# Masked sums inside the experts' work, one select for two heads, and the end stage's buffers in two pools

## The chip, the core and the metric

The kernel runs on one core of a Trainium2 chip. The metric is the device time of one execution in microseconds (us). Five engines follow their own instruction streams: TensorE (PE, with its weight loads shown as PEld), VectorE (DVE), ScalarE (ACT), GpSimd (POOL) and SyncE (SP, which here only issues DMAs). Times inside one execution are counted from the start of the profiled span.

## The reference

One transformer block in float32 on 2048 tokens of width 512. Attention and the feed-forward part both read the normalised input, and both are added to the input.

```python
xn = layernorm(x)
# attention: 16 heads, each with two score maps of width 16
q, k = rotary(xn @ Wq), rotary(xn @ Wk)
attn1 = softmax(causal(q1 @ k1.T * scale)) @ v        # v is 32 wide
attn2 = softmax(causal(q2 @ k2.T * scale)) @ v
f = rfft(attn1, axis=time) - lambda_full * rfft(attn2, axis=time)
attn = irfft(f * exp(-0.5 * (linspace(0, 1, n_freq) / 0.15) ** 2), axis=time)
attn = attn * rsqrt(mean(attn * attn, over each head) + 1e-5) * rms_weight * (1 - LAMBDA_INIT)
# feed forward: 8 experts 352 wide, the best 2 for each token, and a shared one 704 wide
y = sum over the token's 2 experts of weight * (silu(xn @ w1) * (xn @ w3)) @ w2
shared = (silu(xn @ sw1) * (xn @ sw3)) @ sw2
return x + attn @ Wout + y + shared
```

## The kernel before

**Stages.** A first stage normalises the input, routes the tokens to the experts and makes queries, keys and values. The middle stage runs from about 100 to 1240 us: attention on all heads, and between its steps the feed-forward part, so that PE always has one of the two to do. The end stage finishes the filter along time, normalises, multiplies by `Wout` and adds everything up. Middle and end are hand-ordered: PE, DVE, ACT and POOL execute in the order in which the code emits their instructions. Only SP's DMAs are placed by a scheduler.

**Attention.** The heads go in 8 groups `g` of two, and each group in 4 chunks of 512 queries, from the last (`qc` = 3) to the first. A chunk is a list of units. In a unit PE makes a 128 x 2 x 512 tile of scores (`ps_s`, line 822), ACT takes its exponential into a `pt` tile (line 835), PE multiplies `pt` with the values into `ps_o` (line 862), and DVE adds `pt` up into `sum0` or `sum1` for the denominator (lines 876 and 879). Five units of each chunk lie on the diagonal and are masked: POOL zeroes one triangle of 128 columns of `pt` for each part of a unit (the select, line 840). Two of these units cover one key block each for the two heads, two pack two parts, and the last one holds the same key block for both heads, at columns 0 and 256. A group has 29 + 21 + 13 + 5 = 68 units.

**Closing a chunk.** When all units are multiplied, PE sums `sum0` and `sum1` over partitions (line 888), transposes the result, and DVE takes the reciprocal `rcp` (line 903) and scales (`o_n`, line 908). POOL then adds the two maps into `vd` (`put`, line 917). The transposed denominators share PSUM banks with other work of PE, among it the experts' `xy`, so PE can wait for `rcp`.

**Fold steps.** Once a group's four chunks are done, its part of the transform along time is done on POOL by `folded` (lines 928 to 970), a generator with 8 steps of 2, 2, 4, 5, 5, 6, 5 and 3 instructions between its yields. The main loop runs 0, 1 or 2 such steps at the end of an iteration.

**The main loop** takes four units at a time. It emits two units' scores, products with values, the sums of a closing chunk, two more units' scores, more products, the put and the reciprocals of chunks that end; then it alternates `work()`, a step of the generator of the feed-forward part, with `added(...)`, the sums on DVE; last come the fold steps. In each step of `work()` there are DVE instructions of the experts too, and POOL issues the gather `xrow` of the tokens of a coming tile (line 623).

**The end stage** opens the pools `tail1` (the matrices of the filter, `wo_sb`) and `tail` (all else). It begins with the last part of the shared expert: `wh` (PE), `ws` (ACT line 256, DVE lines 257 and 263). Then come products with 23 matrices (`ps_r`, `ps_z`, lines 1141), `first` on ACT (line 1184), the sums `vd` on DVE (lines 1186 and 1187, which combine `ps_r` and `first`), and so on. Meanwhile the residual tiles `res` are prepared for 16 tiles of tokens: SP loads the input (line 1120), POOL issues a DMA that accumulates the shared expert's result `ysh` on it (line 1123) and two indirect DMAs that accumulate the routed experts' rows from `ys` (line 1125). Twelve `res` buffers exist; the last four tiles are prepared as buffers come free (`still`).

**The closing loop** runs over n = 0 to 7, with two tiles of tokens in each round. `prepared(n+2)` makes `y` on DVE (line 1163) and its square `sq` on ACT (line 1219); `means` reduces `sq` to `ms` on DVE (line 1223) and asks ACT for the root; `scales` makes `rms` and then `a` (line 1234) on DVE; `across` transposes `a` on PE (`ps_tr`, line 1262) and copies it to `aT` on ACT (line 1264); `projected` multiplies with `wo_sb` (`po`, line 1270); `finished` adds `po` to `res` on DVE (line 1275) and stores it. At n = 1 the shared expert's last tile is copied out of PSUM (`y_sb`).

A pool's tile at an address waits for all users of older tiles at this address, and the first tile of a pool opened in place of older ones waits for the users of all of the region that the pool covers.

Of the kernel before, what the change touches and what calls it, by code (L numbers as in the profile page):

```python
# [8 lines left out]
F32 = mybir.dt.float32  # L9
# [4 lines left out]
ALU = mybir.AluOpType  # L14
AX = mybir.AxisListType
PSUM = bass.MemoryType.PSUM
# [3 lines left out]
P = 128  # L20
T = 2048
E = 512
# [45 lines left out]
def block_kernel(  # L68
# [527 lines left out]
    def middle(general):  # L596


        with ExitStack() as pools:
# [157 lines left out]
            def greatest(g, qc):  # L757
# [28 lines left out]
                nc.vector.tensor_copy(shift, ps.rearrange("p t q -> p (t q)"))  # L786
                return shift

            class Chunk:


# [19 lines left out]
                def scores(self, unit):  # L811

                    g, qc = self.g, self.qc
                    if general and not self.probs:
                        self.shift = greatest(g, qc)
                    ps = sps.tile([P, 2, QC], F32, tag="sc", name="ps_s")
                    for h, kb, off, col, w in unit:
                        for s in range(2):
                            r = slice(64 * s, 64 * s + 64)
                            k = keys[2 * g + h, kb // TQ][r, kb % TQ * P : (kb % TQ + 1) * P]  # L820
                            to = ps[:, s, col : col + w]
                            nc.tensor.matmul(  # L822
                                to, k, queries[2 * g + h, qc][r, off : off + w], start=True, stop=not general
                            )
                            if general:
                                r = 64 * h + 32 * s
                                nc.tensor.matmul(
                                    to, ones[r : r + 1, :], self.shift[r : r + 1, off : off + w],
                                    start=False, stop=kb < qc * TQ,
                                )  # L830
                                if kb >= qc * TQ:
                                    nc.tensor.matmul(to[:, :P], identb, mask, start=False, stop=True)
                    pt = pp.tile([P, 2, QC], F32, tag="pt", name="pt")
                    used = slice(min(c for *_, c, _ in unit), max(c + w for *_, c, w in unit))
                    nc.scalar.activation(pt[:, :, used], ps[:, :, used], AF.Exp, scale=SCALE)  # L835
                    for _, kb, _, col, _ in unit:
                        if kb >= qc * TQ and not general:

                            part = pt[:, :, col : col + P]
                            nc.gpsimd.affine_select(  # L840
                                out=part, in_=part, pattern=[[0, 2], [1, P]], compare_op=ALU.is_ge, fill=0.0,
                                base=0, channel_multiplier=-1,
                            )
                    ready = []
                    for h, kb, off, col, w in unit:
                        self.probs[h, kb] = pt[:, :, col : col + w], off
                        if (1 - h, kb) in self.probs:
                            ready.append((self, kb))
                    return ready
# [163 lines left out]
            def work():  # L1013
                nonlocal worked
                worked += next(ex, work_all)

            def masked(entry):
                _, c, unit = entry
                return any(kb >= c.qc * TQ for _, kb, *_ in unit)

            def added(entries):

                for n, c, unit in entries:
# [5 lines left out]
            for i in range(0, len(stream), 4):  # L1029
                units = stream[i : i + 4]  # L1030
                found = burst(units[:2])
                n, ended = values()
                for c in closing:
                    c.sums()
                    summed += 1
                if n < 2 and not closing:

                    work()
                found += burst(units[2:])
                while todo:  # L1040
                    ended += values()[1]
                todo += found
                for c in closed:
                    c.put(nc.gpsimd)
                    if c.qc == 0:
                        ready.append(c.g)
                closed, closing = closing, ended
                for c in closed:
                    c.finish()
                held, before = [], held  # L1050
                added(before)
                added(u for u in units[:2] if not masked(u))
                later = [u for u in units[2:] if not masked(u)]
                while True:
                    work()
                    added(later[:1])
                    later = later[1:]
                    if worked / (work_all - left) >= (i + 4) / len(stream):
                        break
                added(later)  # L1060
                added(u for u in units if masked(u))
                if any(map(masked, units)) or not shared:
                    steps = 0
                else:
                    steps = 1 if any(map(masked, stream[i + 4 : i + 8])) else 2
                for _ in range(steps):
                    if folding is None and ready:
                        folding = folded(ready.pop(0), nc.gpsimd)
                    if folding is not None and next(folding, 0) == 0:
                        folding = None  # L1070
# [20 lines left out]
    def ending():  # L1091

        with tc.tile_pool(name="tail1", bufs=1) as t1, tc.tile_pool(name="tail", bufs=2) as tp, tc.tile_pool(
            name="tail_ps", bufs=4, space=PSUM
        ) as fps, tc.tile_pool(name="conv_ps", bufs=2, space=PSUM) as zps, tc.manual_schedule(
            engines={mybir.EngineType.PE, mybir.EngineType.DVE, mybir.EngineType.Activation, mybir.EngineType.Pool}
        ):
            conv = t1.tile([P, CONVS * P], F32, name="conv")  # L1100
            nc.scalar.dma_start(conv[:, : 11 * P], conv_t[:, : 11 * P])
            nc.scalar.dma_start(conv[:, 11 * P :], conv_t[:, 11 * P :])
            _, _, _, _, (_, _, stored), _ = expert(tp, fps)
            hidden, gated, times, _, result = shared_expert(tp, fps, 2)
            fetch_down(wex[NX + 1 : NX + 2], 1, nc.scalar)
            wo_sb = t1.tile([P, NE, E], F32, name="wo_sb")
            nc.scalar.dma_start(wo_sb, wout.rearrange("(c p) e -> p c e", p=P))
# [8 lines left out]

            def fetched(k, step):
                if step == 0:
                    res = tp.tile([P, E], F32, tag="res", name="res", bufs=12)
                    nc.sync.dma_start(res, query[0, order[k] * P : (order[k] + 1) * P, :])  # L1120
                    came.append(res)
                elif step == 1:
                    nc.gpsimd.dma_start(came[k], ysh[order[k]], accum_op=ALU.add)
                else:
                    nc.gpsimd.indirect_dma_start(  # L1125
                        out=came[k], out_offset=None, in_=ys,
                        in_offset=bass.IndirectOffsetOnAxis(ap=slot[:, step - 2, order[k] : order[k] + 1], axis=0),
                        compute_op=ALU.add,
                    )
# [20 lines left out]
                return z  # L1150

            def copied(z):
                diff = tp.tile([P, 2, E], F32, tag="diff", name="diff")
                nc.scalar.copy(diff, z)
                return diff

# [23 lines left out]
            zr = pair("ps_r")  # L1180
            product(zr[:, 0, :], [(0, vd[:, 0, :])])
            product(zr[:, 1, :], [(1, vd[:, 1, :])])
            first = tp.tile([P, E], F32, tag="first", name="first", bufs=1)
            nc.scalar.copy(first, zr[:, 1, :])
            z4 = at(0, fold, 2)
            nc.vector.tensor_add(low[:, 0], zr[:, 0, :], first)
# [86 lines left out]
            def finished(k, po):  # L1273
                res = came[k]
                nc.vector.tensor_add(res, res, po)
                nc.sync.dma_start(out_t[:, order[k], :], res)
# [35 lines left out]
            for n in range(NT // 2):  # L1312
                after = across(2 * n + 1)
                ahead, po = po, projected(aT)
                if n + 1 < NT // 2:
                    pairs[n + 1].scales()
                if n == 1:
                    stored(y, ysh[NT - 1], 0.5)
                if n + 1 < NT // 2:
                    aT = across(2 * n + 2)  # L1320
                if n + 2 < NT // 2:
                    pairs.append(prepared(n + 2))
                if ahead is not None:
                    finished(2 * n - 1, ahead)
                    still(2 * n - 1)
                if n + 2 < NT // 2:
                    pairs[n + 2].means()
                if n + 1 < NT // 2:
                    now, po = po, projected(after)
                    finished(2 * n, now)  # L1330
                    still(2 * n)
# [138 lines left out]
```

## Time and profile before

| | us |
|---|---|
| median of 3 runs | 1359.56 |
| the three runs | 1359.56, 1356.74, 1360.22 |
| the profiled execution | 1360.14 |
| its span, first to last instruction | 1358.3 |
| PE busy | 1312.6 |
| DVE busy | 1005.4 |
| ACT busy | 688.4 |
| POOL busy | 626.3 |
| mean granted clock of PE | 0.994 of full speed |

The profile page and the answers of the trace use lines of this form: start, duration, engine, line, operation, output<-input with sizes, a count, and in brackets the idle time just before with what ended it (the releaser, seen from semaphores). A list of waits gives the engine, its instruction's line, what it waited for, the microseconds in total, how many times, and the longest. Windows give for each stretch the busy time of each engine with its count of instructions, the granted clock, the DMA share and the DMA rate in GB/s.

### The profile page before, as it was taken

What the parts mean: (1) busy time and instruction counts of PE and PEld (TensorE: products, weight loads), DVE (VectorE), ACT (ScalarE), POOL (GpSimd) and SP (SyncE); (2) the same over time, 40 slices, a digit from 0 to 9 for tenths busy, and PEclk for the clock granted to TensorE, in tenths of its full rate; (3) what the DMA queues carried; (4) which work ended last, traced back from release to release, by engine and by line L of the source; (5) the groups of instructions that cost most, each with busy time, mean ns of one, the idle gap of its engine ahead of it and who ended that gap; (6) DMA issues with size and microseconds to landing.
All of it is one profiled execution on the core that took longest, in us unless ns stands there. A gap on an engine that the chain in (4) does not pass through costs nothing.

```text
span 1358.3 us, 20810 instructions
## 1 busy us (share of the span) xinstructions
PE 1312.6 (97%) x7554; PEld 600.3 (44%) x7554; DVE 1005.4 (74%) x1344; ACT 688.4 (51%) x847; POOL 626.3 (46%) x671
## 2 busy tenths in 40 slices
PE   7999999999999999999999999899999999987998
PEld 3444444334443444445444444344544444443544
DVE  7049883287668778868889986778898788764785
ACT  2311110265656566676666666566676666640221
POOL 0002330012221323235968984778589469421764
PEclk9999999999999999999999999999999999998999
DMA  9406673200211122235665656555565666777997
GB/s 375 171 16 171 201 196 97 89 15 32 75 43 31 40 75 82 74 123 170 190 194 143 226 176 180 181 173 174 185 194 178 210 189 230 262 294 293 175 219 169
DMA packets 75578, 214.29 MB, mean 158 GB/s; under 512 B 12244, under 2 KB 12696, under 8 KB 69576
## 3 DMA queue, kind: packets, MB, share of 16 engines
q1 hardware_dynamic: 62744, 185.68, 41.7%
q0 software_dynamic: 11056, 22.78, 8.6%
q10 hardware_dynamic: 1664, 4.38, 0.9%
q8 instruction: 63, 1.03, 0.3%
q14 instruction: 51, 0.42, 0.1%
HBM read 169.69 MB, written 43.10 MB: 157 GB/s over the span
## 4 chain that ended last, share of the span: by engine, by line
PE 65%; DVE 6%; POOL 5%; DMA 3%; issue 1%; ACT 1%; SPq 0%; DVEq 0%; ACTq 0%; POOLq 0%
PE ps_o L862 16%; PE ps_s L822 12%; PE wh L246 8%; PE xy L216 6%; PE xg L180 5%; PE xh L180 5%; PE wy L284 4%; PE ps_sum L888 2%; DMA wu<-in_wex_dram 2%; POOL pt L840 1%; PE po L1270 1%; DMA wd<-in_wex_dram 1%; DVE sum L879 1%; PE ps_ot L900 1%; PE ps_x L165 1%
## 5 line engine op out<-in xcount | busy, mean ns | idle before, releaser
L879 DVE TENSOR_TENSOR sum<-sum,pt 128x1024 f32<-128x1024 f32 (+3 forms) x576 | 621.4, 1128 | 36.3 <-ACT pt L835 21.6
L835 ACT ACTIVATE pt<-ps_s 128x1024 f32<-128x1024 f32 x544 | 527.3, 1023 | 184.3 <-PE ps_s L822 131.0
L840 POOL TENSOR_SCALAR_AFFINE_SELECT pt<-pt 128x256 f32<-128x256 f32 x256 | 171.0, 693 | 358.7 <-ACT pt L835 357.5
L862 PE MATMUL ps_o<-pt,vd 128*32 128x512 f32 (+3 forms) x2560 | 268.0, 534 | 4.1 <-POOL pt L840 4.1
L822 PE MATMUL ps_s<-qS,kS 64*128 64x512 f32 (+3 forms) x1280 | 203.8, 406 | 2.0 <-DVEq L1335 1.6
L822 PEld LDWEIGHTS ps_s<-qS,kS 64*128 64x128 f32 x1280 | 97.1, 185 | 177.0 <-issue 95.9
L246 PE MATMUL wh<-xnT,wu 128*128 128x512 f32 (+1 forms) x352 | 150.4, 574 | 0.0
L862 PEld LDWEIGHTS ps_o<-pt,vd 128*32 128x32 f32 x2560 | 66.9, 109 | 125.8 <-issue 103.5
L545 PE MATMUL ps_x<-xnT,wqk_sb 128*128 128x512 f32 x256 | 110.5, 593 | 0.0
L498 POOL DMA_INDIRECT who<-pairs,slot x32 | 33.1, 1034 | 165.9 <-DVE pairs L495 104.9
L216 PE MATMUL xy<-wd,uT 128*128 128x512 f32 (+3 forms) x240 | 97.1, 606 | 7.7 <-DVE rcp L903 6.3
L246 PEld LDWEIGHTS wh<-xnT,wu 128*128 128x128 f32 x352 | 64.1, 190 | 72.7 <-issue 56.5
L180 PE MATMUL xh<-wu,xT 128*128 128x352 f32 (+1 forms) x320 | 90.5, 473 | 4.2 <-DMA wu<-in_wex_dram 3.3
L917 POOL TENSOR_TENSOR vd<-o_n 128x128 f32<-128x128 f32 x60 | 62.2, 1057 | 65.6 <-DVE o_n L908 65.5
L180 PE MATMUL xg<-wu,xT 128*128 128x352 f32 (+1 forms) x320 | 88.6, 468 | 0.0
L545 PEld LDWEIGHTS ps_x<-xnT,wqk_sb 128*128 128x128 f32 x256 | 48.4, 190 | 60.6 <-issue 60.6
L284 PE MATMUL wy<-wd,ws 128*128 128x512 f32 x160 | 74.8, 603 | 0.0
L257 DVE SCALAR_TENSOR_TENSOR ws<-ws,wh 128x512 f32<-128x512 f32 (+4 forms) x26 | 16.7, 644 | 73.6 <-ACT ws L256 73.6
L1125 POOL DMA_INDIRECT res<-ys,slot x32 | 54.9, 1715 | 25.3 <-DMA res<-ysh 13.5
L562 ACT CAST hi<-turned 128x1024 fp32r<-128x1024 f32 x16 | 16.7, 1045 | 93.9 <-DVE turned L560 70.9
L180 PEld LDWEIGHTS xh<-wu,xT 128*128 128x128 f32 (+1 forms) x320 | 48.0, 176 | 31.7 <-issue 6.5
L180 PEld LDWEIGHTS xg<-wu,xT 128*128 128x128 f32 (+1 forms) x320 | 46.6, 174 | 34.4 <-issue 14.8
(254 smaller groups left out, 1416.8 us busy)
## 6 DMA issues: line engine op xcount, KB each, us to landing
wu<-in_wex_dram SPq DMA_DIRECT2D x44, 1408.0 KB
wd<-in_wex_dram SPq DMA_DIRECT2D x43, 768.0 KB
kS<-parts_k SPq DMA_DIRECT2D x128, 128.0 KB
qS<-parts_q SPq DMA_DIRECT2D x256, 64.0 KB
ys<-y_sb SPq DMA_DIRECT2D x34, 256.0 KB
parts_q<-hi SPq DMA_DIRECT2D x32, 256.0 KB
parts_k<-hi SPq DMA_DIRECT2D x16, 256.0 KB
parts_k<-turned SPq DMA_DIRECT2D x16, 256.0 KB
```

What stands on the lines that cost most here:

```text
L180: nc.tensor.matmul(dst[r, :], xT[:, c, r], w[:, o : o + FI], start=(c == 0), stop=(c == NE - 1), skip_group_check=True,)
L216: nc.tensor.matmul(y[r, :], uT[:m, ic, r], w[:m, ic * E : (ic + 1) * E], start=(ic == 0), stop=(ic == NF - 1), skip_group_check=True,)
L246: nc.tensor.matmul(dst, w_sb[o // WUP][0][:, o % WUP : o % WUP + P], x[:, c, :], start=(c == 0), stop=(c == NE - 1))
L284: nc.tensor.matmul(y, us[i][:, t * P : (t + 1) * P], w_sb[i // NF][1][:, i % NF * E : (i % NF + 1) * E], start=(i == 0), stop=(i == SCH - 1),)
L545: nc.tensor.matmul(ps[:, i, :], wqk_sb[st, qk][:, i, c, :], xnT[:, c, cols], start=(c == 0), stop=(c == NE - 1),)
L822: nc.tensor.matmul(to, k, queries[2 * g + h, qc][r, off : off + w], start=True, stop=not general)
L835: nc.scalar.activation(pt[:, :, used], ps[:, :, used], AF.Exp, scale=SCALE)
L840: nc.gpsimd.affine_select(out=part, in_=part, pattern=[[0, 2], [1, P]], compare_op=ALU.is_ge, fill=0.0, base=0, channel_multiplier=-1,)
L862: nc.tensor.matmul(self.o[r : r + 32, off:], vd[:, kb, v0 : v0 + 32], pt[:, s, :], start=first, stop=self.ended, skip_group_check=True,)
L879: nc.vector.tensor_add(to, to, pt)
L917: eng.tensor_add(vd[:, self.qc * TQ : (self.qc + 1) * TQ, v0 : v0 + 32], self.o_n[:, :, h, 0, :], self.o_n[:, :, h, 1, :],)
L1125: nc.gpsimd.indirect_dma_start(out=came[k], out_offset=None, in_=ys, in_offset=bass.IndirectOffsetOnAxis(ap=slot[:, step - 2, order[k] : o ...
```

## The change

- `masked` becomes a function of a chunk and a unit, in front of the class, and `Chunk.scores` uses it. Where the unit's columns are exactly 0 and 256, one select takes both triangles as 4 blocks of 128 columns.
- In the main loop the sums of a masked unit among the first two of an iteration are emitted behind its first `work()` and ahead of the first of the later unmasked ones. Before, all masked units' sums came last.
- Ahead of an iteration with masked units, a fold step is run only if another group waits to be folded (`ready`), or in the last group. Before, one step was always run there.
- In the end stage the `res`, `ws` (and the other tiles of the shared expert's last part), `first` and `diff` tiles go to a pool of their own, `tail2`; the rest stays in `tail`. All tiles keep their addresses.
- The shared expert's last row tile is copied by ACT in place of DVE.
- In the closing loop `finished(2n - 1)` and `still(2n - 1)` come ahead of `across(2n + 2)` and `prepared(n + 2)`.

```diff
--- before.py
+++ after.py
@@ -786,6 +786,9 @@
                 nc.vector.tensor_copy(shift, ps.rearrange("p t q -> p (t q)"))
                 return shift
 
+            def masked(chunk, unit):
+                return any(kb >= chunk.qc * TQ for _, kb, *_ in unit)
+
             class Chunk:
 
 
@@ -833,13 +836,17 @@
                     pt = pp.tile([P, 2, QC], F32, tag="pt", name="pt")
                     used = slice(min(c for *_, c, _ in unit), max(c + w for *_, c, w in unit))
                     nc.scalar.activation(pt[:, :, used], ps[:, :, used], AF.Exp, scale=SCALE)
-                    for _, kb, _, col, _ in unit:
-                        if kb >= qc * TQ and not general:
-
-                            part = pt[:, :, col : col + P]
+                    if masked(self, unit) and not general:
+
+                        cols = [col for *_, col, _ in unit]
+                        if cols == [0, 2 * P]:
+                            chosen = [pt.rearrange("p s (h q) -> p (s h) q", h=2)[:, :, :P]]
+                        else:
+                            chosen = [pt[:, :, col : col + P] for col in cols]
+                        for part in chosen:
                             nc.gpsimd.affine_select(
-                                out=part, in_=part, pattern=[[0, 2], [1, P]], compare_op=ALU.is_ge, fill=0.0,
-                                base=0, channel_multiplier=-1,
+                                out=part, in_=part, pattern=[[0, part.shape[1]], [1, P]], compare_op=ALU.is_ge,
+                                fill=0.0, base=0, channel_multiplier=-1,
                             )
                     ready = []
                     for h, kb, off, col, w in unit:
@@ -1014,10 +1021,6 @@
                 nonlocal worked
                 worked += next(ex, work_all)
 
-            def masked(entry):
-                _, c, unit = entry
-                return any(kb >= c.qc * TQ for _, kb, *_ in unit)
-
             def added(entries):
 
                 for n, c, unit in entries:
@@ -1049,20 +1052,24 @@
                     c.finish()
                 held, before = [], held
                 added(before)
-                added(u for u in units[:2] if not masked(u))
-                later = [u for u in units[2:] if not masked(u)]
+                added(u for u in units[:2] if not masked(*u[1:]))
+                later = [u for u in units[2:] if not masked(*u[1:])]
+                looked = [u for u in units[:2] if masked(*u[1:])]
                 while True:
                     work()
+                    added(looked)
                     added(later[:1])
-                    later = later[1:]
+                    later, looked = later[1:], []
                     if worked / (work_all - left) >= (i + 4) / len(stream):
                         break
                 added(later)
-                added(u for u in units if masked(u))
-                if any(map(masked, units)) or not shared:
+                added(u for u in units[2:] if masked(*u[1:]))
+                if any(masked(*u[1:]) for u in units) or not shared:
                     steps = 0
+                elif any(masked(*u[1:]) for u in stream[i + 4 : i + 8]):
+                    steps = 1 if ready or units[0][1].g == NG - 1 else 0
                 else:
-                    steps = 1 if any(map(masked, stream[i + 4 : i + 8])) else 2
+                    steps = 2
                 for _ in range(steps):
                     if folding is None and ready:
                         folding = folded(ready.pop(0), nc.gpsimd)
@@ -1092,16 +1099,18 @@
 
 
 
-        with tc.tile_pool(name="tail1", bufs=1) as t1, tc.tile_pool(name="tail", bufs=2) as tp, tc.tile_pool(
-            name="tail_ps", bufs=4, space=PSUM
-        ) as fps, tc.tile_pool(name="conv_ps", bufs=2, space=PSUM) as zps, tc.manual_schedule(
+        with tc.tile_pool(name="tail1", bufs=1) as t1, tc.tile_pool(name="tail2", bufs=2) as t2, tc.tile_pool(
+            name="tail", bufs=2
+        ) as tp, tc.tile_pool(name="tail_ps", bufs=4, space=PSUM) as fps, tc.tile_pool(
+            name="conv_ps", bufs=2, space=PSUM
+        ) as zps, tc.manual_schedule(
             engines={mybir.EngineType.PE, mybir.EngineType.DVE, mybir.EngineType.Activation, mybir.EngineType.Pool}
         ):
             conv = t1.tile([P, CONVS * P], F32, name="conv")
             nc.scalar.dma_start(conv[:, : 11 * P], conv_t[:, : 11 * P])
             nc.scalar.dma_start(conv[:, 11 * P :], conv_t[:, 11 * P :])
-            _, _, _, _, (_, _, stored), _ = expert(tp, fps)
-            hidden, gated, times, _, result = shared_expert(tp, fps, 2)
+            _, _, _, _, (_, _, stored), _ = expert(tp, fps, by_scalar=True)
+            hidden, gated, times, _, result = shared_expert(t2, fps, 2)
             fetch_down(wex[NX + 1 : NX + 2], 1, nc.scalar)
             wo_sb = t1.tile([P, NE, E], F32, name="wo_sb")
             nc.scalar.dma_start(wo_sb, wout.rearrange("(c p) e -> p c e", p=P))
@@ -1116,7 +1125,7 @@
 
             def fetched(k, step):
                 if step == 0:
-                    res = tp.tile([P, E], F32, tag="res", name="res", bufs=12)
+                    res = t2.tile([P, E], F32, tag="res", name="res", bufs=12)
                     nc.sync.dma_start(res, query[0, order[k] * P : (order[k] + 1) * P, :])
                     came.append(res)
                 elif step == 1:
@@ -1150,7 +1159,7 @@
                 return z
 
             def copied(z):
-                diff = tp.tile([P, 2, E], F32, tag="diff", name="diff")
+                diff = t2.tile([P, 2, E], F32, tag="diff", name="diff")
                 nc.scalar.copy(diff, z)
                 return diff
 
@@ -1180,7 +1189,7 @@
             zr = pair("ps_r")
             product(zr[:, 0, :], [(0, vd[:, 0, :])])
             product(zr[:, 1, :], [(1, vd[:, 1, :])])
-            first = tp.tile([P, E], F32, tag="first", name="first", bufs=1)
+            first = t2.tile([P, E], F32, tag="first", name="first", bufs=1)
             nc.scalar.copy(first, zr[:, 1, :])
             z4 = at(0, fold, 2)
             nc.vector.tensor_add(low[:, 0], zr[:, 0, :], first)
@@ -1316,13 +1325,13 @@
                     pairs[n + 1].scales()
                 if n == 1:
                     stored(y, ysh[NT - 1], 0.5)
+                if ahead is not None:
+                    finished(2 * n - 1, ahead)
+                    still(2 * n - 1)
                 if n + 1 < NT // 2:
                     aT = across(2 * n + 2)
                 if n + 2 < NT // 2:
                     pairs.append(prepared(n + 2))
-                if ahead is not None:
-                    finished(2 * n - 1, ahead)
-                    still(2 * n - 1)
                 if n + 2 < NT // 2:
                     pairs[n + 2].means()
                 if n + 1 < NT // 2:
```

## The prediction

> **What bounds the kernel now.** First the busy shares and the list of what TensorE (PE) waited for, over the whole span of 1358.3 us.
>
> ```profile
> PE 1312.6 (97%) x7554; PEld 600.3 (44%) x7554; DVE 1005.4 (74%) x1344; ACT 688.4 (51%) x847; POOL 626.3 (46%) x671
> ...
> PE xy L216 <- DVE rcp L903: 6.3, 4, 3.3
> PE ps_o L862 <- POOL pt L840: 4.1, 4, 1.6
> PE xh L180 <- DMA wu<-in_wex_dram: 3.3, 2, 2.7
> PE ps_tr L1262 <- DVE a L1234: 2.7, 3, 1.3
> PE ps_z L1141 <- DVE vd L1187: 2.6, 1, 2.6
> PE wh L246 <- DMA wu<-in_wex_dram: 2.3, 1, 2.3
> PE po L1270 <- DVE res L1275: 2.1, 2, 1.9
> ```
>
> PE is busy for 1312.6 us, and the order of its 13857 instructions is the same in both programs. So the change can only move PE's idle time, 45.7 us, and the slow matmuls behind a pause. The last two columns are counts and the longest wait; no entry is large, and the edits touch several at once.
>
> Next the end stage, in the timelines of PE and ScalarE (ACT) and the windows from 1250 us (busy time and count of PE, PEld, DVE, ACT, POOL, then the granted clock).
>
> ```profile
> 1243.60 3.60 PE L1141 MATMUL ps_z<-xnT,conv 128*128 128x512 f32 x8
> 1249.75 15.67 PE L1141 MATMUL ps_z<-xnT,conv 128*128 128x512 f32 x32 [2.55 <-DVE vd L1187]
> 1265.26 3.60 PE L1141 MATMUL ps_z<-vd,conv 128*128 128x512 f32 x8
> ...
> 1247.12 0.38 ACT L256 ACTIVATE ws<-wh 128x256 f32<-128x256 f32 x1 [5.39 <-DMA ys<-y_sb]
> 1247.40 0.58 ACT L1184 COPY first<-ps_r 128x512 f32<-128x512 f32 x1
> ...
> 1250.00:1254.00 4.00, 4.00 (x6) 1.56 (x6) 2.06 (x2) 0.00 (x0) 1.41 (x3) 0.57 1.05 392
> ```
>
> ACT stands 5.39 us until the last expert tile's store (ys<-y_sb) has landed, then makes `ws` and `first`; DVE's two `vd` sums follow and PE has run dry for 2.55 us. Behind the pause the granted clock is 0.57 and only six matmuls start in 4 us.
>
> Last, two places of the body where GpSimd (POOL) or VectorE (DVE) is just in time, and one round of the closing loop.
>
> ```profile
> 1048.11 4.81 POOL L970 TENSOR_TENSOR vd<-vd 128x128 f32<-128x128 f32 x1
> 1053.08 5.39 POOL L623 DMA_INDIRECT xrow<-xd,tok  x1 [0.16 <-issue]
> 1058.49 0.77 POOL L840 TENSOR_SCALAR_AFFINE_SELECT pt<-pt 128x256 f32<-128x256 f32 x2
> ...
> 1088.79 4.08 DVE L879 TENSOR_TENSOR sum<-sum,pt 128x768 f32<-128x768 f32 x6
> 1092.93 0.26 DVE L903 RECIPROCAL rcp<-ps_st 128x16 f32<-128x16 f32 x1
> ...
> 1317.61 1.22 DVE L1163 SCALAR_TENSOR_TENSOR y<-xnT,vd 128x1024 f32<-128x1024 f32 x1
> 1318.74 0.68 DVE L1275 TENSOR_TENSOR res<-res,po 128x512 f32<-128x512 f32 x1
> 1320.07 1.22 DVE L1223 TENSOR_REDUCE ms<-sq 128x32 f32<-128x1024 f32 x1 [0.65 <-ACT sq L1219]
> ```
>
> The first masked product of that group starts on PE at 1058.77, with its select at 1058.49: no slack. PE's `xy` starts at 1093.25, right behind the `rcp` that the six sums hold up: no slack either. In the loop the `res` add lies in the time in which DVE waits for ACT's `sq` anyway.
>
> **Part A, the end stage's buffers in two pools.** The addresses stay the same. What changes is what a pool's first tile waits for: the new pool lies over attention's query and probability buffers alone, the old one over the experts' output tiles. So `ws` and `first` no longer wait for the store. PE's `ps_r` ends at 1241.78 + 1.98 = 1243.76; `first` takes 0.58, the `vd` sums 0.68 each: ready at about 1245.7, while PE is in `ps_z` until 1247.20. The 2.55 us go. The clock: the 32 matmuls go from start 1249.75 to 1265.26, 15.51 us, against 0.43 each in the undisturbed products of `po` (8 from 1290.86 to 1294.30): 13.76. So 1.75 more, A = −4.3. What is late next is `vd` itself, 1.45 us behind its limit; DVE waits 6.6 us for PE behind it, so DVE follows. The other end is −1: ACT issues the `wo_sb` load ahead of nothing but these two, and that load now waits for the sixth `res` load. No DMA moved between 1238 and 1242 us, so I take that one as landed at ACT's issue (1241.79); if the added loads push it to 1245, little is left.
>
> The row shows the slow clock behind 2.55 us without matmuls. The Trainium skill, "TensorE: Matmul & The Clock Gate", Part 1, puts the return to half clock after an idle window of about 3.4 us; by that the 1.75 would not belong to this pause and the sum would stand 1.75 higher. The measured 0.57 decides.
>
> **Part B, what the pools let start early.** Three `res` loads (0.79 MB) move on SyncE's (SP) queue ahead of the two `wu` fetches of 1224.18, seven behind the `wd` fetches of 1228.98 and two behind the last store; before, all 12 were issued from 1247.16. They wait for the conv landing near 1220.7 and for transfers that were due then. The queue behind them is `wu`, `ys`, `wd`, and PE waits for these (2.34 us at 1230.42). In 1222–1224 DMA moved 27 GB/s and in 1224–1226 96, so three loads at about 400 fit the hole: 0; without it they cost 0.79 MB / 402 GB/s = 1.9. Three accumulates on POOL's queue (again 0.79 MB) now run beside `wu` and `wd`: at the 255 GB/s of 1236–1238 that is up to 3.1. The four accumulates issued from 1252.59 landed only for the gather at 1260.42, after the backlog of other queues (392 GB/s) was through; so they give way, and I take 0. Bounds of B: 0 and +5.
>
> **Part C, the closing loop's sums in another order.** The odd `res` add goes ahead of `y`. In before it filled the wait for `sq`; now `y`, `sq`, `ms` and `a` come later by its 0.6 us from start to start. At n=1 the slot of `y_sb` (0.60 at 1299.06), which goes to ACT (0.69 in a stage where ACT is mostly idle), is free for it: 0. From n=2 each round adds 0.6. The transposes at 1317.74 already wait 1.27 us for `a`: +0.6. In round 3 (+1.2) `a` ends 1.1 us ahead of its transposes: absorbed. Those at 1333.95 wait 0.50: +1.8 in all. In round 5 (+2.4) `a` would end at 1343.06 and its transposes, themselves 1.8 later, start at 1343.56: absorbed. C = +1.8, bounds 0 (where `a` isn't what PE waits for) and +2.4.
>
> **Part D, the body.** In 32 chunks two selects of 256 elements become one of 512. Alone a select takes 0.37 to 0.41, beside DVE's sums 0.83; the one of 512 isn't in the trace; bounds are 0.6 and 2 × 0.83, at most a gain of 0.2 each. The products that PE waits for (4.1 us in all) need the selects before it, so I count 0. DVE's swaps lie within one set of sums between two `rcp`: 0; the same `rcp` end the waits of 6.3.
>
> The fold steps on POOL come later: their number is the same. At 1041.58 eleven narrow adds stand where eight stood. The eight took 11.34 us because single adds last 4.81 us while DVE's sums run; the eleven, at 0.3 to 0.5 alone, end some 1.0 later if the pauses between the sums take most, 4.2 later in proportion (11.34 × 3/8). Behind them queue the `xrow` gather and the select of 1058.49, which PE and DVE await: +1.0, bounds 0 and +4.2. At 1088 eight narrow adds stand beside the six sums where POOL stood idle. With the same eight adds the six took 5.04 at 972.65; beside adds of 512 wide at 846.67, 7.59; idle 4.08. So +1.0, bounds 0 and +3.5. At 979 eleven adds come in front of two wide ones that go later; the selects at 994.19 may be up to 2 us late, but PE uses them at 999.00: 0, bounds 0 and +1. Steps ahead of selects get fewer at 1031; PE didn't wait there: 0. The bound below is that all 4.1 us of waits for POOL go, since DVE's moved sums leave the selects their 0.4: −4.1. D = +2.0, from −4.1 to +8.7.
>
> The Trainium skill, "SBUF — State Buffer", "two separate sides", calls the port pair that DVE and POOL share an exclusive lock for a whole instruction; this speaks against the moved steps. If each of the three added ones at 1041 waited for a whole sum (1.2 us, as in the pairs of 2.34), they would cost 3.6 in place of 1.0, and the sum would stand 2.6 higher.
>
> **Sum.** −4.3 + 0 + 1.8 + 2.0 = −0.5, against the profiled run of 1360.14 us (span 1358.3 and 1.8 around it): 1359.6. The median of the three runs, 1359.56, lies 0.6 lower: 1359.1. A measurement of this kernel tells about 0.3%, 4.1 us, from no change, so this is no change.
>
> **Rivals.** *Faster, 1353.0.* The fold steps hide (D without the +2.0) and the waits for POOL at 755, 758, 883 and 1119 go: −4.3 + 1.8 − 4.1 = −6.6. For it: selects of 0.83 against 0.41, so six of them lose 2.5 us beside DVE's sums. Against: at these places the fold steps ahead and the sums beside are the same. It counts as faster once 1.6 of the 4.1 go with D otherwise nil.
> *Slower, 1365.8.* The moved fold steps collide with the sums in front of an `rcp` or a select: at the upper bounds of 1041, 1088 and 979, 8.7 in place of 2.0, −0.5 + 6.7 = +6.2. It decides from +6.6 on in D (−4.3 + 1.8 + 6.6 = +4.1). For it: no slack at 1058.77 and 1093.25. Against: these steps are narrow, and POOL is idle 54% of the span.
> *The pools don't free ACT, 1363.4.* ACT stands at `wo_sb` for a `res` load: A is nil, +3.8, still within 0.3%.
>
> **How the numbers follow.** Forecast 0.35, third rival 0.05, faster 0.33, slower 0.27. The forecast's own range is 1355.6 to 1363. Faster by over 0.3% 0.33, within 0.40, slower 0.27. The range reaches to 1351.5 (the faster rival and 1 us of C) and 1366.5 (the slower one and a little of B); beyond each I leave about one in ten.
>
> **What would show it.** A: no wait of PE near 1249, a clock of 1.0 behind it, `first` near 1244. B: the waits for `wu` and `wd` near 1230 and 1238 as before. C: the longer wait for `sq` in the closing loop, and waits for `a` of about 1.9 and 1.7 us. D: the six sums near 1088 at about 5 us with a wait of about 1 us for `rcp` behind them, and a wait for a select near 1059. I am wrong if PE's waits for POOL or `rcp` in the body change by more than 3 us in sum, or if PE stands at 1249 as before.

## The result and the profile after

| | before | changed |
|---|---|---|
| median of 5 runs, us | 1359.56 | 1367.70 |
| lowest and highest, us | 1356.33, 1360.67 | 1365.80, 1370.80 |
| profiled execution and its span, us | 1360.14, 1358.3 | 1370.8, 1369.0 |

The ratio is 1.0072 with a 95% interval from 1.0050 to 1.0094; by the medians the changed kernel is 8.1 us slower. The forecast was 1359.1, no change, and the range to 1366.5 doesn't hold the result. The profiled execution of the changed kernel is the slowest of its five, so its terms sum to some 2.6 us more than the medians show.

First the busy shares of the changed kernel, to be laid beside those of before (the profiles of both hold 7554 matmuls and 7554 weight loads of PE; the prediction's 13857 instructions stand in neither):

```profile
PE 1317.5 (96%) x7554; PEld 602.5 (44%) x7554; DVE 1010.6 (74%) x1343; ACT 689.1 (50%) x848; POOL 607.4 (44%) x639
```

And PE's list of waits in it (line numbers have moved by up to 9):

```profile
...
PE xy L216 <- DVE rcp L910: 7.9, 4, 3.7
PE xy L216 <- DMA wd<-in_wex_dram: 4.7, 1, 4.7
PE ps_o L869 <- POOL pt L847: 4.6, 5, 1.6
PE wh L246 <- DMA wu<-in_wex_dram: 4.6, 1, 4.6
PE ps_tr L1271 <- DVE a L1243: 3.6, 2, 2.6
```

The wait for `vd` (2.6 us) is gone, and in its place stands one for `wd` (4.7; 0.7 in before), while the one for `wu` has doubled. PE's order of matmuls is the same in both, so each matmul's start can be laid beside its own in the other profile, and the delay tells where the time went:

| place (start in the changed kernel) | what delayed PE | delay, us |
|---|---|---|
| 256 to 260 | four matmuls at half clock behind a pause that both have | +1.7 |
| 856 | `rcp`, wait 3.67 in place of 3.27 | +0.4 |
| 1002 to 1004 | a late select, 0.50 of it as a listed wait | +1.5 |
| 1098 | `rcp`, wait 1.31 in place of none | +1.4 |
| 1237 to 1244 | `wu`, wait 4.60 in place of 2.34, and half clock behind it | +3.2 |
| 1248 to 1253 | `wd`, wait 4.66 in place of 0.70, and half clock behind it | +5.2 |
| 1260 to 1263 | no wait for `vd`, full clock | −4.5 |
| 1321 to 1345 | `a`, wait 2.64 in place of 1.27 (+1.4), half clock behind it (+1.7), less of two other waits (−1.1) | +2.0 |

The first row lies ahead of all that the change moves: the first select starts only at 280.75. Some of the kernels of the experiments have this slow clock and some don't.

The fetches first. The timeline of SP's queue in the changed kernel, each line with its start, the time over which the DMAs were issued, and how many:

```profile
1225.77 1.44 SPq L1129 DMA_DIRECT2D res<-in_query_dram  x3
1229.01 0.80 SPq L146 DMA_DIRECT2D wu<-in_wex_dram  x2
...
1233.81 0.94 SPq L149 DMA_DIRECT2D wd<-in_wex_dram  x2
1234.79 13.79 SPq L1129 DMA_DIRECT2D res<-in_query_dram  x7
```

And POOL's:

```profile
1230.66 2.84 POOL L1132 DMA_DIRECT2D res<-ysh  x3 [13.63 <-DMA res<-in_query_dram]
```

`wu` is asked for at 1229.01, 4.83 us later than in before (1224.18), which is just the delay of the body: the loads ahead of it on SP's queue cost it nothing. But POOL issues the three accumulates 1.6 us behind it, and PE gets `wu` 8.5 us after the issue, against 6.2. The windows of this stretch (PE, PEld, DVE, ACT, POOL, then clock, DMA share, GB/s):

```profile
1236.00:1238.00 2.00, 0.49 (x2) 0.49 (x3) 1.86 (x11) 0.00 (x0) 0.00 (x0) 0.50 1.05 300
1238.00:1240.00 2.00, 2.00 (x11) 2.00 (x11) 1.90 (x9) 0.00 (x0) 0.00 (x0) 0.50 0.94 233
1240.00:1242.00 2.00, 2.00 (x12) 2.00 (x11) 1.79 (x9) 0.00 (x0) 0.00 (x0) 0.50 1.10 277
```

And in before, where `wu` and `wd` came:

```profile
1226.00:1236.00 10.00, 7.34 (x43) 5.65 (x39) 8.11 (x32) 0.69 (x1) 0.00 (x0) 0.83 0.98 402
```

The DMA engines are as good as always busy in these three windows of the changed kernel and yet move only 233 to 300 GB/s, against 402 in before. The trace's packets tell why. A packet of an accumulate (2048 bytes) holds a DMA engine for 183 ns on average, a packet of the same size of a plain load for 86. The three accumulates are 384 packets, 4.4 us of all 16 engines, and they run between 1235 and 1247, among the packets of `wu` and `wd`; the two `wu` fetches take 12.7 us from their first packet to their last in place of 8.2.

Now the fold steps. The timeline of POOL around the first place:

```profile
999.98 4.16 POOL L847 TENSOR_SCALAR_AFFINE_SELECT pt<-pt 128x256 f32<-128x256 f32 x6
```

PE's, where a product waits for the fifth or sixth of these selects:

```profile
1004.20 0.41 PE L869 MATMUL ps_o<-pt,vd 128*32 128x128 f32 x4 [0.50 <-POOL pt L847]
```

And DVE's at the second place:

```profile
1092.87 2.77 DVE L886 TENSOR_TENSOR sum<-sum,pt 128x768 f32<-128x768 f32 x3
1096.09 1.98 DVE L886 TENSOR_TENSOR sum<-sum,pt 128x256 f32<-128x256 f32 x3 [0.45 <-POOL vd L973]
1097.99 0.25 DVE L910 RECIPROCAL rcp<-ps_st 128x16 f32<-128x16 f32 x1
```

The selects that started at 994.19 start at 999.98. Behind the shift of 2.2 us that the body had by then they are 3.6 us late. The six sums take 5.20 us from the start of the first to the end of the last, against 4.08, and `rcp` holds PE for 1.31 us.

Last the closing loop, on PE:

```profile
1327.26 0.66 PE L1271 MATMUL ps_tr<-cst,a 128*128 128x128 f32 x4 [2.64 <-DVE a L1243]
1327.76 5.29 PE L1279 MATMUL po<-wo_sb,aT 128*128 128x512 f32 x8
```

The transposes wait 1.37 us longer than before, and the eight products behind them take 5.29 us where such a group takes 3.60.

### The profile page after: what moved, and what is told of

Same layout as the page of the kernel before. It is cut to its first block, busy times and chain, and to the rows that moved or that the text cites. A ratio compares the mean times of both kernels' runs of the same rounds, so it can differ in the third digit from the quotient of the medians.

```text
span 1369.0 us, 20779 instructions
## 1 busy us (share of the span) xinstructions
PE 1317.5 (96%) x7554; PEld 602.5 (44%) x7554; DVE 1010.6 (74%) x1343; ACT 689.1 (50%) x848; POOL 607.4 (44%) x639
## 4 chain that ended last, share of the span: by engine, by line
PE 59%; POOL 9%; DMA 8%; DVE 4%; issue 2%; SPq 1%; ACT 1%; DVEq 0%; POOLq 0%; ACTq 0%
PE ps_o L869 15%; PE ps_s L825 11%; PE wh L246 8%; PE xy L216 5%; PE xh L180 5%; PE xg L180 5%; PE wy L284 4%; DMA wd<-in_wex_dram 3%; PE po L1279 2%; DMA kS<-parts_k 2%; POOL pt L847 2%; DMA wu<-in_wex_dram 2%; PE ps_sum L895 1%; DVE sum L886 1%; POOL vd L924 1%
## 5 line engine op out<-in xcount | busy, mean ns | idle before, releaser
L886 DVE TENSOR_TENSOR sum<-sum,pt 128x1024 f32<-128x1024 f32 (+2 forms) x576 | 624.7, 1135 | 22.0 <-POOL pt L847 8.8
L847 POOL TENSOR_SCALAR_AFFINE_SELECT pt<-pt 128x256 f32<-128x256 f32 (+1 forms) x224 | 162.7, 748 | 385.8 <-ACT pt L838 384.6
L216 PE MATMUL xy<-wd,uT 128*128 128x512 f32 (+3 forms) x240 | 99.1, 621 | 12.7 <-DVE rcp L910 7.9
L924 POOL TENSOR_TENSOR vd<-o_n 128x128 f32<-128x128 f32 x60 | 55.1, 938 | 60.5 <-DVE o_n L915 60.5
L257 DVE SCALAR_TENSOR_TENSOR ws<-ws,wh 128x512 f32<-128x512 f32 (+4 forms) x26 | 16.7, 644 | 79.2 <-ACT ws L256 79.2
L562 ACT CAST hi<-turned 128x1024 fp32r<-128x1024 f32 x16 | 16.7, 1045 | 93.9 <-DVE turned L560 59.4
L225 ACT ACTIVATE y_sb<-xy,wcol 128x512 f32<-128x512 f32 x34 | 23.4, 688 | 79.3 <-PE xy L216 79.3
```

What stands on the lines that cost most here:

```text
L216: nc.tensor.matmul(y[r, :], uT[:m, ic, r], w[:m, ic * E : (ic + 1) * E], start=(ic == 0), stop=(ic == NF - 1), skip_group_check=True,)
L847: nc.gpsimd.affine_select(out=part, in_=part, pattern=[[0, part.shape[1]], [1, P]], compare_op=ALU.is_ge, fill=0.0, base=0, channel_multip ...
L886: nc.vector.tensor_add(to, to, pt)
L924: eng.tensor_add(vd[:, self.qc * TQ : (self.qc + 1) * TQ, v0 : v0 + 32], self.o_n[:, :, h, 0, :], self.o_n[:, :, h, 1, :],)
```

## The experiments

Each kernel was run on the chip beside the kernel before; ratios are to that one, with their 95% intervals. Two theories stood at the start. Theory 1: the transfers cost most, that is the early `res` DMAs. Theory 2: the body costs most, and the waits for `wu` and `wd` belong to the profiled execution alone. Differences in us between two changed kernels are differences of medians; the kernel before, run beside each of them, had medians from 1359.0 to 1360.0. The intervals of the ratios are 0.1 to 0.2% on each side, some 1.5 to 3 us, so the matched starts of the profiles are needed beside them.

**Early `res` undone.** The changed kernel with

```diff
-                    res = t2.tile([P, E], F32, tag="res", name="res", bufs=12)
+                    res = tp.tile([P, E], F32, tag="res", name="res", bufs=12)
```

> The changed kernel, with the res tiles alone back in the pool over the experts' tiles, so that their loads and accumulates start behind the last expert store again. Theory 1 (transfers): the early loads and accumulates took the DMA engines from the wu and wd fetches and cost about 8 us; without them this kernel stands at 1359 to 1361, with waits for wu and wd of about 2.3 and 1.5 us as in before. Theory 2 (body): the moved fold steps and sums cost most, and the long waits for wu and wd belong to the profiled execution; this kernel stands at 1364 or above.

Measured: 1359.03, ratio 1.0000 [0.9987, 1.0013]. That is 8.7 us less than the changed kernel. PE's list shows 2.3 us for `wu` and 0.7 for `wd`. Theory 1 holds for the early `res` DMAs as a whole.

**Fold steps undone.** The changed kernel with

```diff
-                elif any(masked(*u[1:]) for u in stream[i + 4 : i + 8]):
-                    steps = 1 if ready or units[0][1].g == NG - 1 else 0
                 else:
-                    steps = 2
+                    steps = 1 if any(masked(*u[1:]) for u in stream[i + 4 : i + 8]) else 2
```

> The changed kernel with the fold steps where they were before. Theory 1: the waits for a select near 1004 and for rcp near 1098 go, about 2.3 to 3.3 us, and this kernel stands at 1364 to 1366. Theory 2: the fold steps are the main cost; 1359 to 1362.

Measured: 1363.98, ratio 1.0032 [1.0019, 1.0045], 3.7 us less than the changed kernel. In the profile the delays at 1004 and 1098 are gone, 1.5 and 1.2 us against the changed kernel. That is at the lower edge of theory 1 and outside theory 2.

**The closing loop undone.** The changed kernel with `finished(2n - 1)` and `still(2n - 1)` behind `prepared(n + 2)` again:

```diff
-                if ahead is not None:
-                    finished(2 * n - 1, ahead)
-                    still(2 * n - 1)
                 if n + 1 < NT // 2:
                     aT = across(2 * n + 2)
                 if n + 2 < NT // 2:
                     pairs.append(prepared(n + 2))
+                if ahead is not None:
+                    finished(2 * n - 1, ahead)
+                    still(2 * n - 1)
```

> The changed kernel with the closing loop's sums in the order of before. Theory 1: the odd sum ahead of y delays a by 1.4 to 2 us in all, so this kernel stands at 1365.5 to 1366.5, and the wait for a of 2.6 us falls to about 1.3. Rival: the new order spares waits for res and costs nothing; 1367.5 to 1369.

Measured: 1365.75, ratio 1.0051 [1.0033, 1.0070], 1.95 us less than the changed kernel, and the longest wait for `a` is back at 1.3 us. The interval is wide against so small a difference; the wait is what settles it.

**The pools alone.** The kernel before with `tail2` opened and only these moved to it:

```diff
-            hidden, gated, times, _, result = shared_expert(tp, fps, 2)
+            hidden, gated, times, _, result = shared_expert(t2, fps, 2)
...
-                diff = tp.tile([P, 2, E], F32, tag="diff", name="diff")
+                diff = t2.tile([P, 2, E], F32, tag="diff", name="diff")
...
-            first = tp.tile([P, E], F32, tag="first", name="first", bufs=1)
+            first = t2.tile([P, E], F32, tag="first", name="first", bufs=1)
```

> The kernel before, with ws, first and diff in a pool of their own and nothing else changed (res stays behind the last expert store). Theory 1: the wait for vd of 2.55 us and the 1.75 us of slow clock behind it go: 4.3 us less than before, 1355 to 1356 where before is at 1359.5. Rival: the transfers or DVE's chain hold the stage and the gain is lost further on; 1358 to 1360.

Measured: 1355.49, ratio 0.9971 [0.9959, 0.9982], as theory 1 had it. PE's timeline of this kernel shows the products in one run, with no pause where 2.55 us stood:

```profile
1241.79 1.98 PE L1143 MATMUL ps_r<-vd,conv 128*128 128x512 f32 x4 [0.83 <-ACT y_sb L225]
1243.61 12.61 PE L1143 MATMUL ps_z<-xnT,conv 128*128 128x512 f32 x29
```

**Accumulates held.** To part loads from accumulates: the changed kernel, all loads issued as before in it, and POOL held until `first` is there.

```diff
-            for some in (range(4), range(4, 12)):
-                for step in range(4):
-                    for k in some:
-                        fetched(k, step)
+            for k in range(12):
+                fetched(k, 0)
...
             nc.scalar.copy(first, zr[:, 1, :])
+            hold = tp.tile([P, 1], F32, tag="hold", name="hold", bufs=1)
+            nc.gpsimd.tensor_scalar(hold, first[:, :1], 1.0, None, ALU.mult)
+            for some in (range(4), range(4, 12)):
+                for step in range(1, 4):
+                    for k in some:
+                        fetched(k, step)
```

> The changed kernel with the early res loads kept, and POOL's accumulates and gathers held until ACT has made first (by one POOL instruction on one column of first). Theory L (the loads alone take the DMA engines from wu and wd): 1366 to 1368 and waits for wu and wd as long as in the changed kernel. Theory S (the accumulates, which read and write the same tile, take most): 1360 to 1362, with the waits back near 2.3 and 1.5 us.

Measured: 1362.06, ratio 1.0018 [1.0006, 1.0031], 5.6 us less than the changed kernel and at the edge of theory S. PE's waits in this stretch are 2.2 us for `wu`, and 2.3 us for the fold on DVE where `wd` held PE:

```profile
PE xy L216 <- DVE vd L973: 2.3, 1, 2.3
PE wh L246 <- DMA wu<-in_wex_dram: 2.2, 1, 2.2
```

Against the kernel with `res` late (1.0000 [0.9987, 1.0013]) 3 us were left, which a later run takes up.

**Four tiles early.** The changed kernel with eight of the twelve buffers in the old pool:

```diff
-                    res = t2.tile([P, E], F32, tag="res", name="res", bufs=12)
+                    early = k % 12 < 4
+                    pool, tag = (t2, "res") if early else (tp, "res_late")
+                    res = pool.tile([P, E], F32, tag=tag, name="res", bufs=4 if early else 8)
```

> The changed kernel with only the first four res buffers in the new pool; the loads of the other eight start behind the last expert store. What moves early is then four loads and three or four accumulates. If the seven loads issued behind wd delay it, the wait for wd near 1248 (4.7 us) falls to about 1 and the kernel stands at 1362 to 1364; if the accumulates do, it stays at 1366 to 1368.

Measured: 1367.55, ratio 1.0053 [1.0032, 1.0073]. The wait for `wd` stays, with one load in place of seven behind it on SP's queue; that for `wu` is 2.2 us here, so the cost has moved from one fetch to the other. From PE's list of waits:

```profile
PE xy L216 <- DMA wd<-in_wex_dram: 5.6, 1, 5.6
```

POOL's timeline has the accumulates where the changed kernel has them:

```profile
1228.38 2.85 POOL L1134 DMA_DIRECT2D res<-ysh  x3 [13.53 <-DMA res<-in_query_dram]
```

So it is three accumulates, not ten early loads, that cost the time. In the four kernels that have the accumulates early, 16.7 to 17.6 us pass from PE's first `wh`, the product that waits for `wu`, to the end of the experts' last `xy`; in before and in the kernel with `res` late it is 10.5 and 10.7, with the accumulates held 11.5.

**Three things undone together.** The changed kernel with the first three edits of this section.

> The changed kernel with three things undone together: early res, moved fold steps, new order in the closing loop. If the three costs add up (8.7, 3.7 and 1.9 us by the single runs), 1353 to 1354; if they overlap, 1355 to 1357. Against the pools alone (1355.5) it also shows what the select for two heads, the earlier masked sums and y_sb on ACT are worth together: about -2 if they add up, 0 if they are hidden.

Measured: 1356.50, ratio 0.9980 [0.9967, 0.9992]. The three costs add up to 14.3 us singly and 11.2 together, which is in the range for overlap; but the runs scatter by 2 us, so how much of the 3 us is overlap stays open. Against the pools alone (0.9971) the select for two heads, the earlier masked sums and `y_sb` on ACT gain nothing.

**The pools and the select.** The kernel with the pools alone, and the one select for two heads.

> The kernel with the pools alone, and the one select for two heads besides. By the prediction the select is hidden: 1355 to 1356, as the pools alone. Rival: it frees POOL for the selects that PE waits for (4.1 us in all) and the kernel stands at 1352 to 1354.

Measured: 1356.05, ratio 0.9969 [0.9957, 0.9981]: hidden, as the prediction had it. Its profile has the wait for `rcp` near 855 at 3.69 us in place of 3.27, like the changed kernel's: POOL is done with its selects sooner and starts the wide fold adds sooner beside DVE's sums.

**A better place for the fold steps.** The case at 846 us in before, where wide fold adds stretch six sums to 7.59 us, and the cost of the moved steps at 1098 point to one rule: no fold step in an iteration in which a chunk ends, since DVE then adds what `rcp` waits for. In before:

```profile
846.67 7.59 DVE L879 TENSOR_TENSOR sum<-sum,pt 128x768 f32<-128x768 f32 x6
```

On the kernel with the pools alone:

```diff
                     steps = 1 if any(map(masked, stream[i + 4 : i + 8])) else 2
+                if closing:
+                    steps = 0
```

> The kernel before with the pools alone, and no fold step in an iteration in which a chunk ends, since DVE then adds the last sums ahead of its rcp. If wide fold adds beside these sums are what delays rcp, the six sums near 846.7 fall from 7.6 us to about 4, PE's wait of 3.3 us there and the slow clock behind it go (4 to 5 us) and the kernel stands at 1350.5 to 1352. Rival: the steps run into the selects instead and PE waits there; 1355 to 1358.

Measured: 1346.78, ratio 0.9900 [0.9883, 0.9917]: 13.2 us faster than before, 8.7 more than the pools alone by the medians, and faster than was expected. DVE's timeline:

```profile
843.44 4.09 DVE L879 TENSOR_TENSOR sum<-sum,pt 128x768 f32<-128x768 f32 x6
847.59 0.26 DVE L903 RECIPROCAL rcp<-ps_st 128x16 f32<-128x16 f32 x1
```

And PE's list of waits:

```profile
PE xy L216 <- DVE rcp L903: 2.9, 2, 1.4
...
PE ps_o L862 <- POOL pt L840: 1.7, 2, 0.9
```

The six sums are back at 4.09 us, and the wait of 3.27 us goes with the slow clock behind it: 5.0 us at 848, as expected. What was not expected is 3.0 us more near 755: six selects, which in the kernel with the pools alone started at 753.15 and took 5.07 us beside DVE's sums, start at 751.41 and take 2.19, done as DVE's sums begin, so PE's two waits there go too. Near 874 0.6 are saved. The rule settles the two largest collisions of the body at once.

**Early loads without accumulates.** The kernel with the pools, `res` in the new pool, and the hold from above.

> The kernel before with the pools, res in the new pool too, so that its loads start early, and POOL's accumulates held until first is made; loop, fold steps and selects as in before. If the early loads alone cost nothing, it stands with the pools alone, 1355 to 1356; if they cost a third of the 8 us, 1358 to 1359.

Measured: 1356.71, ratio 0.9977 [0.9966, 0.9988], against 0.9971 [0.9959, 0.9982] for the pools alone: 0.06% with intervals of 0.1% on each side. The early loads alone cost little or nothing, and they bring nothing either. The 3 us left above are therefore not the loads' in the main. In the end stage the profile of the kernel with the accumulates held, laid beside that of the one with `res` late, has 0.8 us more at the fetches and 2.0 more at 1295, where a wait for `res` that both have (2.0 and 1.7 us) is followed by a slow clock in one and not in the other. Whether other executions show the same isn't known, so what the 3 us are stays open.

**The select once more.** The kernel with the better fold rule, and the one select.

> The kernel with the pools alone and no fold step where a chunk ends (1346.8), and the one select for two heads besides. PE still waits 1.7 us for selects there. If the select is hidden, 1346 to 1348; if it shortens these waits, 1344.5 to 1345.5.

Measured: 1347.52, ratio 0.9919 [0.9904, 0.9933]. Hidden here too.

## Why the prediction was wrong

The step that failed is part B, "so they give way, and I take 0". It cost 8.7 us by the kernel without it, and 8.4 in the matched starts of the profiles (+3.2 and +5.2), beyond its bound of +5. The row that it was read from is this, in before:

```profile
1252.59 3.72 POOL L1123 DMA_DIRECT2D res<-ysh  x4 [40.08 <-DVE vd L1190]
```

That the gather behind these four accumulates started only at 1260.42, 7.8 us after the first issue, was read as their giving way to other transfers. But by the trace's packets the first one starts 4.4 us after that issue (1256.98), and in the changed kernel the first packet again starts 4.4 us after the issue (1230.66 to 1235.09); in all 13 profiles it is 3.2 to 4.5 us. So more than half of the 7.8 us is a delay ahead of the first packet, and it comes wherever the accumulates stand. Nothing that PE waited for ran beside them in before, so the row could not show what they do to others either.

The bound of +5 was too low for two more reasons. The accumulates' price was taken by bytes (0.79 MB at 255 GB/s, 3.1 us); their packets hold all 16 engines for 4.4 us, twice the time of a load. And a longer pause of PE has a slow clock behind it, here 0.9 us behind `wu` and, less a second wait that only before has there, 1.3 behind `wd`. The two waits themselves grew by 6.2 us; why by more than 4.4 isn't shown.

- **A, the pools.** Right, −4.3 forecast; −4.0 by the medians and −4.5 in the profile, in its two parts.
- **B, the loads.** That three loads fit in the hole is borne out as to cost (early loads alone 0.9977 against 0.9971), though the hole is then no hole any more: 306 and 248 GB/s in the two windows that had 27 and 96.
- **C, the closing loop.** +1.8 forecast, +1.95 measured (profile +2.0). The path was a little other: in the changed kernel the wait near 1327 grew by 1.4, not 0.6, and brought a slow clock, and that near 1345 went. In the kernel with `res` late both waits grew by 1.1 and no slow clock came.
- **D, the fold steps.** +2.0 forecast, +3.7 measured by undoing them (profile about 3). The term at 1088 was right in its mechanism and measured +1.4 for +1.0. The one at 1059, +1.0, didn't come: the select started at 1061.79, 3.3 us later than in before and so no later than the body's delay of 3.7; the fold adds ended later, but the `xrow` gather between them and the select is recorded with 1.57 us in place of 5.39. The one at 994, put at 0, cost 1.5: the selects were 3.6 us late, not 2.
- **The select, DVE's swaps.** 0 forecast, nothing measured.

Of the rivals, the slower one came nearest in time (1365.8), but by the wrong mechanism: the fold steps were 3.7 of the loss, the transfers 8.7. The faster rival's waits for POOL didn't go (4.6 us in place of 4.1); the third rival fell, since `first` started at 1257.12 right behind `ps_r`.

The sum with the measured terms is −4.0 + 8.7 + 1.95 + 3.7 = +10.4, against +8.1; the three costs do not add up in full when undone together either.

## What to carry to other kernels

A transfer that is made to start earlier has to be priced in the engines' time for its packets, beside what is in flight for the engine that sets the end; that it was slow elsewhere doesn't mean that it yields. A buffer that comes free early lets in all that waits for it, and here the good part of the edit (ACT freed, −4) and the bad one (accumulates, +8.7) came with one and the same pool. Where two engines slow each other down, put the movable work away from the sums that a waited-for result hangs on: that rule alone was worth twice what the pools were.

## What the runs showed of the hardware

- An accumulate's packet of 2048 bytes holds a DMA engine for 183 ns beside the fetches in the changed kernel and for 176 in the first three accumulates of before; a load's packet of this size, 86 to 89.
- From POOL's issue of the first accumulate to its first packet 3.2 to 4.5 us pass, in all 13 profiles.
- The slow clock comes behind pauses of quite different length, and not each time. PE's pause of 1.6 us near 256 us is followed by some matmuls at 0.85 us in place of 0.43 in 7 of the 13 profiles (7 of the 9 with the one select in their code and none of the 4 without, though the first select starts only at 278 us or later, so this may be chance); one of 2.64 us in the closing loop was, one of 2.39 in the kernel with `res` late was not, nor one of 2.57 in the kernel with the accumulates held. The Trainium skill, "TensorE: Matmul & The Clock Gate", Part 1, calls the activity window free-running and the effect variable from run to run, which agrees; its idle window of about 3.4 us is longer than the pauses of 1.6 to 2.6 us seen here.
- Beside a long run of DVE's sums a narrow POOL instruction of some 0.5 us took 5.09 us (line 963, at 1050.85), as long as four sums, not one. The Trainium skill, "SBUF — State Buffer", "two separate sides", gives the ports that the two share to whichever starts first, for its whole instruction; by that the loser would wait for one sum of 1.2 us, and this row is longer by a factor of four, with the reserve that POOL's spans in the records are rough.
